# A second network for half of the rows set apart, whole VectorE operations in the last pair, and gathers that wait for the last but one

## Chip, cores and metric

One NeuronCore of one Trainium2 chip runs the whole kernel. The metric is the device time of one execution in microseconds, the median of several runs.

## What is computed

For each of 16 graphs of 1024 nodes with 64 features: normalize the rows and clip them at zero (h), drop some neighbours of nodes that have more than ten, take for every node and feature the quantiles 0.25, 0.5 and 0.75 over the neighbours that are left (itself among them), add their weighted sum to h, and put the result through two dense layers. Cut from the reference:

```
neigh = (adj_ > 0) & ~eye
rem = neigh & (sk > 1) & (rank % sk == sk - 1) & mask[:, :, None]
adj_d = jnp.where(rem | jnp.swapaxes(rem, 1, 2), 0.0, adj_)
vals = jnp.where((adj_d > 0)[..., None], x[:, None, :, :], jnp.inf)
s = jnp.sort(vals, axis=2)
for tau, w in zip((0.25, 0.5, 0.75), (0.25, 0.5, 0.25)):
    pos = tau * max(nv - 1, 0); lo, hi = floor(pos), ceil(pos)
    agg = agg + w * (v_lo + frac * (v_hi - v_lo))
y = relu((x + agg) @ W1 + b1) @ W2 + b2
```

Here x is h, nv the number of values of a node, and the layer's input is added to y at the end.

## The kernel before

**Tiling.** Nodes lie on the 128 partitions. TensorE and ScalarE turn each adjacency matrix into short lists of neighbours (`load`, `drop`, `keep`, `order`, `collect`). The nodes are put in order of their number of neighbours, so that eight tiles of 128 nodes need fewer and fewer slots (`CAPS`); `CLASSES` joins tiles with one number of lines: 13, 11, 9 and 7. Two graphs make a pair, and there are eight pairs.

**Gathers.** A slot of a tile of one graph is filled by one indirect DMA from GpSimd (POOL), L1274 in `fetch`: 128 rows of 64 floats out of a table in DRAM (`gtab`) into a tile `g`. A node without a neighbour in that slot gathers a row of the constant BIG.

**Sorting.** `sort` runs over a network written down in `PLANS`. A step is `n` pairs of lines at regular distances. With two results it is a min (L1379) and a max (L1384), each over n lines at once; with one it is L1376. An operation holds at most `PART` = 384 elements for each partition, so two lines of the 11-line class (384 elements each) go as two operations. Only those lines that can carry a quantile come out sorted (`ends`); each is multiplied by its coefficient, by VectorE at L1401 or by ScalarE at L1399 from pair `ACTP` = 3 on, and TensorE adds them up in PSUM (L1405, `acc`). From the last pair the second half is sorted for each graph by itself.

**Writes behind.** `opened` puts a write of one column (`pause`, L801) behind an operation of VectorE. A max writes over lines that its min has read; where at least one instruction stands between the two in VectorE's order, `arrange` declares that there is no dependence (`loose`), and the max need not wait.

**Rows set apart.** The 32 nodes of a graph with the most neighbours don't fit the tiles' slots. Of eight graphs, a group, they fill two rows per partition: the first (k = 0) holds nodes of up to 23 neighbours, the second (k = 1) nodes of up to `SECOND` = 14. `set_apart` copies their first slots into the tile `gg`, and `fetch_group` gathers the others (L1624). Slots that k = 1 doesn't use are filled with BIG by VectorE (L1622). `aggregate_group` sorts both rows together, 128 columns, with the 24-line network, adds the lines up in `gacc`, and goes on through the dense layers (`go`, `ot`, `gh`, `yp` at L1601, `gx`) to a scatter (L1691). There are two groups: the first is sorted in the middle of the kernel, the second ahead of the last pair. The sum of the second is also brought back into the last pair (`bring_back`, `few`).

**Order of the work.** The Python code emits the work of a pair, with the preparation of later graphs woven in (`weave`). `arrange` then takes every instruction with its dependences, gives it a cost and a lag (`Step.cost`; a write behind adds 12 ns to its operation), and plays the five queues PE, ACT, DVE, POOL and SP in time; the order found is fixed on each engine. Of several instructions that are ready the one that was emitted first goes first. `results(m)` holds the end of the work of pair m; for the last pair it starts with `aggregate_group` and the scatter, then `aggregate`. In the last pair a part of the slots (`LEAST`) is filled by TensorE (`pick`, with the one-hot tile `hot` from VectorE) and not by gathers.

Of the kernel before, what the change touches and what calls it, by code (L numbers as in the profile page):

```python
# [40 lines left out]
OP = mybir.AluOpType  # L41
# [46 lines left out]

SPREAD = 160
PART = 384  # L90


FIRST = CAPS[0] - 1
# [546 lines left out]
        return 480, 1500 + by / 300  # L640


def arrange(tc, runs, loose, tails):

    steps, found, number = [], {}, {}
    for ins in list(tc.nc.cur_bb.bb.instructions):
# [63 lines left out]
    while done < len(steps):  # L710
# [25 lines left out]
        for q in ENGINES:  # L736
            while waiting[q] and waiting[q][0][0] <= free[q]:
                heappush(able[q], heappop(waiting[q])[1])

    for steps in sequence.values():  # L740
        alike = iter(sorted((i for s in steps for i in s.tail), key=lambda i: number[i.name]))
        line = [i for s in steps for i in (s.ins, *(next(alike) for _ in s.tail))]
        at = {ins.name: k for k, ins in enumerate(line)}
        for ins in line:
            if ins.name in loose and at[loose[ins.name]] < at[ins.name] - 1:
                tc.declare_no_dep(ins, loose[ins.name], reason="read in order by one engine")
        for ins, then in zip(line, line[1:]):
            tc.add_manual_dep(
                then, ins.name, mybir.DependencyInfo(mybir.DependencyClass.NoSync, mybir.DependencyReason.DATA),
                reason="order of the engine",  # L750
            )
# [3 lines left out]
def list_layer(  # L755
# [42 lines left out]
    def opened(ins):  # L798

        at = len(tails) % 64  # L800
        tails[nc.vector.memset(pause[:, at:at + 1], 0.0).ins.name] = ins.ins.name  # L801
        return ins
# [437 lines left out]

    queue = deque()
    turn = [0]

# [17 lines left out]
    def fetch(m, classes=CLASSES, halves=(0, 1)):  # L1263

        for tiles, slots in classes:
            lo, n = tiles[0], len(tiles)
            held, order = PLANS[slots][:2]

            def begin(h, tiles=tiles, lo=lo, n=n, slots=slots, held=held):
                opening((tiles, slots), m)  # L1270
                nc.scalar.copy(gathered[m, tiles][:, slots - 1, :, h], owns[m][:, lo:lo + n, h])

            def gather(h, slot, k, at, tiles=tiles, lo=lo):
                return nc.gpsimd.indirect_dma_start(  # L1274
                    out=gathered[m, tiles][:, slot, k - lo, h], out_offset=None, in_=tables[2 * m + h][0],
                    in_offset=bass.IndirectOffsetOnAxis(ap=lists[2 * m + h][:, at:at + 1], axis=0),
                    element_offset=tables[2 * m + h][1],
                )

            for h in halves:  # L1280
                queue.append(partial(begin, h))
                for k in tiles:
                    for s, slot in enumerate(order[:FULL[k] + ((k, FULL[k]) in HOSTS)]):
                        if m < pairs - 1 or s >= LEAST[k]:
                            queue.append(partial(gather, h, slot, k, PASSED[k] + s))
# [68 lines left out]
                yield 1.0  # L1354


    def sort(lines, plan, first, coef, acc, by_act=False):

        size = prod(lines.shape[2:])

        def at(first, step, n):
            stop = first + step * (n - 1) + (1 if step >= 0 else -1)
            return lines[:, first:stop if stop >= 0 else None:step or 1]

        _, _, steps, ends, taken = plan
        most = max(1, PART // size)

        def parts(n):
            return [(k, min(most, n - k)) for k in range(0, n, most)]

        for n, a, da, b, db, f, df, back, what in steps:
            run, others = [], []
            for k, many in parts(n):
                pa, pb = at(a + k * da, da, many), at(b + k * db, db, many)
                if f < 0:
                    opened(nc.vector.tensor_tensor(pa if back else pb, pa, pb, OP.min if what == "min" else OP.max))  # L1376
                else:
                    run.append(opened(
                        nc.vector.tensor_tensor(at(f + k * df, df, many), pa, pb, OP.min if what == "<" else OP.max)  # L1379
                    ))  # L1380
            for k, many in parts(n) if f >= 0 else ():
                pa, pb = at(a + k * da, da, many), at(b + k * db, db, many)
                others.append(opened(
                    nc.vector.tensor_tensor(pa if back else pb, pa, pb, OP.max if what == "<" else OP.min)  # L1384
                ))
            loose.update((then.ins.name, ins.ins.name) for ins, then in zip(run, others))
            cost = (0.16 + n * size / 960) * (1 if f < 0 else 2)
            yield cost
        for n in taken:
            now, ends = ends[:n], ends[n:]  # L1390
            for k, many in parts(n):
                some = now[k:k + many]
                v = at(some[0], some[1] - some[0] if many > 1 else 0, many)
                v = v.rearrange("p s (k c) -> p s k c", c=C) if len(lines.shape) == 3 else v
                if by_act:
                    w = coef(first + k, many)
                    for i in range(many):
                        for j in range(v.shape[2]):
                            nc.scalar.activation(v[:, i, j], v[:, i, j], AF.Copy, scale=w[:, i, j:j + 1])  # L1399
                    continue  # L1400
                opened(nc.vector.tensor_tensor(  # L1401
                    v, v, coef(first + k, many)[:, :, :, None].to_broadcast(list(v.shape)), OP.mult
                ))
            settle([
                nc.tensor.matmul(  # L1405
                    acc, ident32, lines[:, s], start=False, stop=(s == now[-1] and not ends), skip_group_check=True
                )
                for s in now
            ])
            first += n  # L1410
            cost = 0.16 + n * size / 960
            yield cost
# [22 lines left out]
    def aggregate(m, o, between=None):  # L1435
# [4 lines left out]
        for half in (0, 1) if last else (1, 0):  # L1440
            parts = CLASSES[2 * half:2 * half + 2][::1 if last else -1]
            for sides in ((0, 1), (1, 2)) if last and half else ((0, 2),):
# [28 lines left out]
                for tiles, slots in parts:  # L1471
                    lo, n = tiles[0], len(tiles)
                    g = gathered[m, tiles]
                    plan = PLANS[slots]
                    if one is None:
                        lines, weigh = g.rearrange("p s n h c -> p s (n h c)"), partial(
                            lambda s, many, lo, n: coef[:, s:s + many, lo:lo + n].rearrange("p s n h -> p s (n h)"),
                            lo=lo, n=n,
                        )
                    else:  # L1480
                        lines, weigh = g[:, :, :, one], partial(
                            lambda s, many, lo, n, h: coef[:, s:s + many, lo:lo + n, h], lo=lo, n=n, h=one
                        )
                    yield from sort(
                        lines, plan, window(tiles, slots)[0], weigh, acc[:, lo - 4 * half:lo - 4 * half + n],
                        m >= ACTP,
                    )
                    if sides[1] == 2:
                        gathered.pop((m, tiles))
# [116 lines left out]
    def fetch_group(grp):  # L1606
# [12 lines left out]
        for k in range(n):  # L1619
            for s, slot in enumerate(s for s in PLANS[CAP][1] if s >= FIRST):  # L1620
                if k and s >= SECOND - FIRST:
                    nc.vector.memset(groups[grp][:, slot, k], BIG)  # L1622
                    continue
                nc.gpsimd.indirect_dma_start(  # L1624
                    out=groups[grp][:, slot, k], out_offset=None, in_=tab,
                    in_offset=bass.IndirectOffsetOnAxis(ap=idx[:, k, s:s + 1], axis=0),
                )
            nc.gpsimd.indirect_dma_start(
                out=xg[:, k], out_offset=None, in_=flat_x,
                in_offset=bass.IndirectOffsetOnAxis(ap=to[:, k:k + 1], axis=0),  # L1630
            )
        gathered["group", grp] = to, xg

    def aggregate_group(grp):
# [6 lines left out]
        tag, bufs = ("mx", 3) if grp == B // GROUP - 1 else ("agg", 2)  # L1641
        acc = psum.tile([P, n, C], F32, name="gacc", tag=tag, bufs=bufs)
        nc.tensor.matmul(acc, ident32, gg[:, CAP - 1], start=True, stop=False, skip_group_check=True)
        yield from sort(
            gg.rearrange("p s k c -> p s (k c)"), PLANS[CAP], window((0,), CAP)[0],
            lambda s, many: coef[:, s:s + many], acc.rearrange("p k c -> p (k c)"),
        )
        o = wk.tile([P, n * C], F32, name="go", tag="lows", bufs=1)
        nc.scalar.copy(o, acc.rearrange("p k c -> p (k c)"))
        yield 0.0  # L1650
# [144 lines left out]
                next(side)  # L1795
        weave(chain(results(m - 1) if m else (), (1.0,)), 140.0 if m else 1.0, side, 85.0 if m < pairs - 1 else 45.0)

    arrange(tc, runs, loose, tails)


def ones_col(pool, nc):
# [5 lines left out]
def window(tiles, n):  # L1807
# [56 lines left out]
        (3, 19, 2, 2, 2, 24, 1, 1, "<"), (2, 7, 3, 5, 16, 2, 4, 0, "<"), (3, 5, 10, 1, 1, 4, 3, 1, ">"),  # L1864
        (1, 20, 0, 17, 0, -1, 0, 0, "max"), (2, 0, 8, 14, -5, 2, -1, 0, ">"),
    ), (17, 9, 1, 14, 2, 15, 7, 5, 4, 24, 19, 26, 23, 25, 10, 6, 21), (3, 2, 2, 2, 2, 2, 2, 2)),
}


# [105 lines left out]
```

## Time and profile before

| | |
|---|---|
| median of 3 runs | 1521.11 us (1520.2 to 1524.35) |
| the profiled execution | 2610.97 us, span 2609.2 us |
| mean granted TensorE clock in it | 0.709 |
| PE, PEld busy | 1220.6, 756.3 us |
| DVE (VectorE) busy | 1224.7 us |
| ACT (ScalarE) busy | 1111.4 us |
| POOL (GpSimd) busy | 966.4 us, 952 + 26 + 4 gathers and 4 scatters among it |
| writes behind (L801) | 2237, 59 ns each as recorded |

The span is the time from the first to the last instruction of one profiled execution; 1.8 us lie around it. That execution took 1.72 times the median of the runs without a profile, so its durations of single instructions can be used, and its idle times only with care. [...]the distance from start to start says what an operation costs in a row of them.

### The profile page before, as it was taken

To read this page: it belongs to the slowest core of one execution; us is meant where nothing else is said; L and a number is where in the kernel's file an instruction comes from. 1 tells how busy PE (TensorE), PEld (TensorE's weight loads), DVE (VectorE), ACT (ScalarE), POOL (GpSimd) and SP (SyncE) were. 2 spreads that over 40 slices of the span, in tenths; PEclk is the share of its full clock that TensorE was granted. 3 is DMA by queue.
4 is the path that set the end of the run, shared out by engine and by line. 5 is a ranking of instruction groups with operands and counts; after the bars stand their busy time and mean duration, and the time that the engine had idled before them with its cause. 6 is when DMAs were issued, how large, how long until landed. Compare 5 with 4: busy or idle time off the path is not lost.

```text
span 2609.2 us, 29583 instructions
## 1 busy us (share of the span) xinstructions
PE 1220.6 (47%) x8971; PEld 756.3 (29%) x8971; DVE 1224.7 (47%) x5963; ACT 1111.4 (43%) x3089; POOL 966.4 (37%) x995
## 2 busy tenths in 40 slices
PE   6144246154807192253816427145392254655536
PEld 4133134032404151142413214033251122353223
DVE  5123168043508371383507704088374171449496
ACT  6244146143606271343606626055482254315355
POOL 1724431653272527324370154702507434420400
PEclk9567578576958595585957758577596566876668
DMA  5222122121213121221212112121212010100100
GB/s 171 62 77 68 39 56 73 33 58 45 56 34 86 28 70 32 62 52 50 59 26 80 42 19 59 26 65 33 51 54 50 16 21 16 32 13 3 22 9 11
DMA packets 128826, 121.62 MB, mean 47 GB/s; under 512 B 95730, under 2 KB 96274, under 8 KB 128658
## 3 DMA queue, kind: packets, MB, share of 16 engines
q1 hardware_dynamic: 97106, 87.29, 11.3%
q0 software_dynamic: 31552, 32.36, 6.4%
q8 instruction: 72, 1.18, 0.2%
q14 instruction: 96, 0.79, 0.1%
HBM read 108.79 MB, written 9.05 MB: 45 GB/s over the span
## 4 chain that ended last, share of the span: by engine, by line
another core or an unknown queue 27%; PE 17%; ACT 17%; issue 16%; DVE 6%; DMA 0%; DVEq 0%; ACTq 0%
PE codeP L1090 3%; PE acc L1405 3%; ACT dist L993 2%; ACT g L1399 2%; ACT kept L1016 2%; ACT sg L906 2%; DVE g L1384 1%; ACT ne L926 1%; PE tp L913 1%; DVE g L1379 1%; PE rk L988 1%; PE rk L983 1%; PE got L1341 1%; ACT waste L1188 1%
## 5 line engine op out<-in xcount | busy, mean ns | idle before, releaser
L1274 POOL DMA_INDIRECT g<-gtab,idx x952 | 921.0, 967 | 1373.9 <-issue 307.7
L1384 DVE TENSOR_TENSOR g<-g 128x256 f32<-128x256 f32 (+1 forms) x675 | 312.0, 484 | 39.0 <-remote 26.6
L1379 DVE TENSOR_TENSOR g<-g 128x256 f32<-128x256 f32 (+1 forms) x675 | 312.8, 486 | 28.8 <-remote 18.9
L993 ACT ACTIVATE dist<-rk,bias 128x512 f16<-128x512 f32 x256 | 170.2, 696 | 314.4 <-remote 215.0
L983 PE MATMUL rk<-kb,cnt 128*128 128x512 bf16 x256 | 121.4, 474 | 349.0 <-ACT dist L993 166.9
L926 ACT ACTIVATE ne<-tp 128x512 fp8e4<-128x512 f32 x248 | 141.0, 605 | 280.3 <-remote 226.3
L994 DVE TENSOR_SCALAR rem<-dist,half 128x1024 bf16<-128x1024 f16 x128 | 63.0, 493 | 402.6 <-ACT dist L993 351.7
L913 PE MATMUL tp<-kb,sg 128*128 128x128 bf16 x1024 | 118.4, 258 | 285.2 <-ACT sg L906 114.7
L988 PEld LDWEIGHTS <-ne 128*128 128x128 fp8e4 x1024 | 97.7, 117 | 414.4 <-issue 396.9
L1090 PE MATMUL codeP<-pack,perm 128*128 128x332 bf16 x1024 | 195.1, 333 | 11.2 <-DVE perm L1065 8.7
L913 PEld LDWEIGHTS <-sg 128*128 128x128 bf16 x1024 | 89.5, 118 | 309.0 <-issue 172.1
L1016 ACT ACTIVATE kept<-kp 128x512 fp8e4<-128x512 f32 x224 | 134.2, 615 | 91.8 <-remote 54.1
L1405 PE MATMUL acc<-g,kf 128*128 128x128 f32 (+2 forms) x472 | 141.2, 432 | 64.5 <-ACT g L1399 45.3
L1399 ACT ACTIVATE g<-g,coef 128x64 f32<-128x64 f32 x560 | 147.5, 350 | 52.2 <-DVE g L1379 21.0
L801 DVE MEMSET pause<- 128x1 bf16 x2237 | 132.0, 59 | 7.0 <-issue 7.0
L988 PE MATMUL rk<-kw,ne 128*128 128x128 fp8e5 x1024 | 128.7, 258 | 0.0
L906 ACT ACTIVATE sg<-at 128x1024 bf16<-128x1024 f32 x121 | 126.5, 1070 | 3.4 <-DMA at<-in_adj_dram 3.4
L1105 DVE MAX8 keys<-codeP 128x8 f32<-128x128 f32 x128 | 38.0, 297 | 186.7 <-ACT own L1100 145.1
L1090 PEld LDWEIGHTS <-perm 128*128 128x128 bf16 x1024 | 97.2, 105 | 89.3 <-DVE perm L1065 25.1
L1511 DVE TENSOR_SCALAR at_p<-iota,node 128x512 bf16<-128x512 f16 x208 | 66.8, 357 | 100.0 <-remote 57.4
L1019 PE MATMUL code<-kw,kept 128*128 128x17 fp8e5 x1024 | 65.5, 173 | 98.9 <-issue 56.6
L1405 PEld LDWEIGHTS acc<-g,kf 128*128 128x128 f32 x472 | 83.4, 218 | 90.0 <-ACT g L1399 57.1
(205 smaller groups left out, 2533.5 us busy)
## 6 DMA issues: line engine op xcount, KB each, us to landing
at<-in_adj_dram SPq DMA_DIRECT2D x122, 512.0 KB
g<-gtab,idx POOLq DMA_INDIRECT x952
xt<-in_x_dram SPq DMA_DIRECT2D x16, 256.0 KB
y<-in_x_dram SPq DMA_DIRECT2D x16, 256.0 KB
gtab<-xt SPq DMA_DIRECT2D x16, 256.0 KB
out_dram<-y SPq DMA_DIRECT2D x14, 256.0 KB
spare<-in_adj_dram SPq DMA_DIRECT2D x6, 512.0 KB
gg<-g SPq DMA_DIRECT2D x32, 48.0 KB
```

The costliest lines, as they stand in the source:

```text
L906: nc.scalar.activation(sg, at, AF.Sign)
L913: run.append(nc.tensor.matmul(tp[:, s], sg[:, m * P:(m + 1) * P], ident16, start=(s == 0), stop=(s == 3 and t // 4 != n), skip_group_check ...
L926: nc.scalar.activation(to, tp, AF.Relu, saturate=False)
L988: run.append(nc.tensor.matmul(rk[:, s * P:(s + 1) * P], ne[:, 4 * n + s, ts], upper, start=False, stop=(s == 3), skip_group_check=True,))
L993: nc.scalar.activation(dist[:, n * HALF:(n + 1) * HALF], rk, AF.Abs, bias=bias[:, t:t + 1])
L1016: nc.scalar.activation(kept[:, 4 * n:4 * n + 4], kp, AF.Relu, saturate=False)
L1090: run.append(nc.tensor.matmul(flat, perm[:, t, k * P:(k + 1) * P], pack[:, t], start=False, stop=(t == NT - 1), skip_group_check=True,))
L1274: return nc.gpsimd.indirect_dma_start(out=gathered[m, tiles][:, slot, k - lo, h], out_offset=None, in_=tables[2 * m + h][0], in_offset=bas ...
L1379: nc.vector.tensor_tensor(at(f + k * df, df, many), pa, pb, OP.min if what == "<" else OP.max)
L1384: nc.vector.tensor_tensor(pa if back else pb, pa, pb, OP.max if what == "<" else OP.min)
L1399: nc.scalar.activation(v[:, i, j], v[:, i, j], AF.Copy, scale=w[:, i, j:j + 1])
L1405: nc.tensor.matmul(acc, ident32, lines[:, s], start=False, stop=(s == now[-1] and not ends), skip_group_check=True)
```

## The change

Four things are done.

- The two rows set apart are sorted one after the other in the code, k = 1 first, each over its own 64 columns: k = 1 with a network of 15 lines that uses the slots of the 24-line plan, k = 0 with the 24-line one. The slots that k = 1 doesn't use are no longer filled with BIG.
- In the sorts of the last pair and of the second group an operation may hold `WHOLE` = 1024 elements, and no write stands behind it.
- Each gather of `fetch` adds one to a semaphore when GpSimd has finished it[...]. In the order that `arrange` found, gather k waits until k - 1 of them have done so, that is, until gather k - 2 is through. Gathers of a group and scatters neither wait nor count.
- The sums of the two rows go to their halves of `gacc` separately.

The new network: 26 steps, of two results 1 x 6 pairs, 1 x 4, 3 x 3, 16 x 2, and 5 steps of one result; 10 lines come out, two at a time.

```diff
 PART = 384
+WHOLE = 1024
...
-def arrange(tc, runs, loose, tails):
+def arrange(tc, runs, loose, tails, paced):
...
+    for k, s in enumerate(s for s in sequence["POOL"] if s.ins.name in paced[1]):
+        if k > 1:
+            paced[1][s.ins.name].wait_op(paced[0], k - 1, "sem-ge")
...
+    paced = nc.alloc_semaphore("issued"), {}
...
             def gather(h, slot, k, at, tiles=tiles, lo=lo):
-                return nc.gpsimd.indirect_dma_start(
+                ins = nc.gpsimd.indirect_dma_start(
...
-                    element_offset=tables[2 * m + h][1],
+                    element_offset=tables[2 * m + h][1], engine_sem=issued,
                 )
+                given_out[ins.ins.name] = ins
+                return ins
...
-    def sort(lines, plan, first, coef, acc, by_act=False):
+    def sort(lines, plan, first, coef, acc, by_act=False, whole=False):
...
-        most = max(1, PART // size)
+        most = max(1, (WHOLE if whole else PART) // size)
+        gap = (lambda ins: ins) if whole else opened
...
-                    opened(nc.vector.tensor_tensor(pa if back else pb, pa, pb, OP.min if what == "min" else OP.max))
+                    gap(nc.vector.tensor_tensor(pa if back else pb, pa, pb, OP.min if what == "min" else OP.max))
...
                     yield from sort(
                         lines, plan, window(tiles, slots)[0], weigh, acc[:, lo - 4 * half:lo - 4 * half + n],
-                        m >= ACTP,
+                        m >= ACTP, last,
                     )
...
                 if k and s >= SECOND - FIRST:
-                    nc.vector.memset(groups[grp][:, slot, k], BIG)
                     continue
...
-        yield from sort(
-            gg.rearrange("p s k c -> p s (k c)"), PLANS[CAP], window((0,), CAP)[0],
-            lambda s, many: coef[:, s:s + many], acc.rearrange("p k c -> p (k c)"),
-        )
+        for k in range(n)[::-1]:
+            yield from sort(
+                gg[:, :, k], PLANS[(CAP, SECOND + 1)[k]], window((0,), CAP)[0],
+                lambda s, many: coef[:, s:s + many, k:k + 1], acc[:, k], whole=grp == B // GROUP - 1,
+            )
...
-    arrange(tc, runs, loose, tails)
+    arrange(tc, runs, loose, tails, paced)
...
+    15: (27, (), (
+        (6, 1, 2, 0, 2, 14, 1, 1, "<"), (4, 15, 2, 14, 2, 2, 2, 1, ">"), (3, 11, 6, 9, 6, 22, -4, 1, "<"),
...
+    ), (12, 15, 13, 21, 11, 26, 22, 20, 5, 18), (2, 2, 2, 2, 2)),
```

The min, the max and the multiplication of `sort` all go through `gap` in place of `opened`; the lines left out do that.

## The prediction

> **What bounds the kernel now.** I read the totals first, then the costliest groups, then stretches of the span, then the chain that ended last. The totals show no engine that is full:
>
> ```profile
> PE 1220.6 (47%) x8971; PEld 756.3 (29%) x8971; DVE 1224.7 (47%) x5963; ACT 1111.4 (43%) x3089; POOL 966.4 (37%) x995
> L1274 POOL DMA_INDIRECT g<-gtab,idx x952 | 921.0, 967 | 1373.9 <-issue 307.7
> L801 DVE MEMSET pause<- 128x1 bf16 x2237 | 132.0, 59 | 7.0 <-issue 7.0
> ```
>
> The profiled execution took 2610.97 us for a span of 2609.2, 1.72 times the median of 1521.11. So shares of its span can't be read as shares of a normal run. Stretches show why (columns: stretch, its length, busy PE, PEld, DVE, ACT, POOL, granted clock, DMA share, GB/s):
>
> ```profile
> 1520.00:1540.00 20.00, 1.57 (x10) 0.71 (x10) 0.00 (x0) 1.07 (x3) 15.12 (x17) 0.50 0.15 27
> 1740.00:1760.00 20.00, 0.00 (x0) 0.00 (x0) 19.64 (x99) 0.00 (x0) 0.00 (x0) 0.50 0.00 0
> 2500.00:2520.00 20.00, 0.00 (x0) 0.00 (x0) 20.00 (x93) 15.85 (x27) 0.00 (x0) 0.50 0.00 1
> 2520.00:2540.00 20.00, 4.04 (x19) 4.05 (x20) 20.00 (x97) 0.00 (x0) 0.00 (x0) 0.50 0.00 0
> 2540.00:2560.00 20.00, 13.98 (x52) 8.93 (x52) 16.26 (x78) 13.33 (x54) 1.94 (x2) 0.78 0.01 4
> ```
>
> While POOL issues gathers in a row (first line), the others nearly stop; when it rests they fill up. A normal run can't be like that: gathers, and the others' work after them, would not fit into 1521 us. There the two must overlap. What each costs is still readable. Gathers are paced by start to start:
>
> ```profile
> 2442.98 0.95 POOL L1274 DMA_INDIRECT g<-gtab,idx  x1 [0.30 <-issue]
> 2444.24 0.94 POOL L1274 DMA_INDIRECT g<-gtab,idx  x1 [0.30 <-issue]
> 2445.48 0.95 POOL L1274 DMA_INDIRECT g<-gtab,idx  x1 [0.30 <-issue]
> ```
>
> 1.25 us each. The 952 gathers with the 26 + 4 of the groups make 982 x 1.25 = 1228 us. The first starts at 69.7 us and some 125 to 160 us of work follow the last (161 here, of which up to 35 are the stop beside the last gathers). 70 + 1228 + 125 to 160 = 1423 to 1458 of the 1521: **in the middle POOL is over nine tenths full, and the end is DVE's.** From 2320 to 2588 DVE is the full engine except beside the last 32 gathers; from 2460 to 2544 it is busy 77.7 of 84 us, with no gather left. The chain that ended last goes through DVE's sorting to 2535.9, then:
>
> ```profile
> 2535.96 6.98 PE gacc L1405 x34
> 2546.65 0.76 PE yp L1597 x4
> 2547.50 0.31 DVE yp L1601
> ```
>
> So DVE work taken out of the last 150 us is worth nearly its own length; after DVE's last sort operation (2588.4) a fixed 20.8 us follow.
>
> [...]operations start 0.212, 0.345 and 0.479 us apart at 128, 256 and 384 elements, that is elements/0.96 + 78 ns, the small write behind included; 256-element ones without it start 0.33 apart (L1602 to the next). The write behind costs about 13 ns, not the 59 of its row. [...]in the first group's sort, alone on DVE, the max starts 0.48 after the min, but the next min, which needs that max, starts 0.59 after it:
>
> ```profile
> 1742.75 0.56 DVE L1379 TENSOR_TENSOR gg<-gg 128x384 f32<-128x384 f32 x1
> 1743.23 0.55 DVE L1384 TENSOR_TENSOR gg<-gg 128x384 f32<-128x384 f32 x1
> 1743.82 0.56 DVE L1379 TENSOR_TENSOR gg<-gg 128x384 f32<-128x384 f32 x1
> ```
>
> I take 0.11 us for a dependence that nothing fills.[...]
>
> **The change, part by part.**
>
> *Group sort.* Before, the 24-line network works on both set-apart rows, 128 columns. From the rows of gg (halved, there are two groups): 64 operations of 384, 28 of 256, 3 of 128, and 1 + 7 multiplications: 65 x 0.479 + 35 x 0.345 + 3 x 0.212 = 43.8 us. After, the same 103 operations have 64 columns, and the 15-line network adds 47 operations and 5 multiplications. In the last group without writes behind (elements/0.96 + 65 ns): 24 lines: 65 x 0.265 + 35 x 0.198 + 3 x 0.132 = 24.6; 15 lines: 2 x 0.465 + 2 x 0.332 + 6 x 0.265 + 37 x 0.198 + 5 x 0.132 = 11.2. Sum 35.8: **8.0 us less**. The two networks touch different columns, so each fills the other's handovers. The nine BIG memsets per group go: 9 x 0.112 = 1.0 us less. Sums on PE: 27 lines of 64 columns for 17 of 128, 54 records for 34; at 0.12 to 0.24 us (the 128x64 records of L1597) 6.5 to 13 us against 7.0, but 20 of them belong to the short network and can run while the long one sorts. Behind it 34 stay: nothing.
>
> *First group.* With writes behind it saves about 43.8 - 37.8 + 1.0 = 7 us of DVE. It lies in the stretch where POOL's gathers set the pace; I take 0, with 0 to 7 for the range.
>
> *Whole operations in the last pair.* Only the 11-line class is cut at PART: 64 operations of 384 and 3 more before, 32 of 768 (0.865 each) and 3 after: 32.1 to 29.1, 3.0 less. The 13-line class loses 34 writes, the two sides of the 9- and 7-line classes 88: 122 x 0.013 = 1.6 less. Multiplications there are ACT's and stay.
>
> *What it gives back.* Without the write, a min and its max stand next to each other whenever nothing else is ready, and then the max waits for the min, 0.11 us, where before no wait was declared. Beside another sort it costs nothing. Alone are the last six steps of the 9-line network (15 steps against 9) on each side: 12 x 0.11 = 1.3 us. The 11-line class alone would lose what merging gave: four 0.479 operations or two of 0.865 + 0.11, 1.92 or 1.95 a step; half of it has the group beside it and the rest can have the next side's networks.
>
> *Pacing.* [...]Behind a waiting gather stand the later gathers, group gathers and scatters in POOL's queue; the sorts wait for them. While k waits, k-1 still has about 1.25 us to run, and a semaphore is seen here within 0.02 to 0.12 us ("issue" pieces of the chain), so the wait should end in time. Nor does the distance of gathers hang on how many are queued: at 69.7 us, after 47 idle us, it is 1.48, 1.26, 1.25, the same as 100 gathers later. Bounds: 0 if hidden; if an increment comes into the distance, 0.04 us x 952 = 38 us; below nothing if it is the run ahead that stops the other engines. I take 0. SP's transfers and their order are not touched.
>
> *Sum.* 8.0 + 1.0 + 3.0 + 1.6 - 1.3 = 12.3 us off DVE's last stretch. Against the profiled 2610.97 that is 2598.7; its excess lies beside gathers, so I subtract the same from the median: 1521.1 - 12.3 = **1508.8, say 1509 us**. The written-out order is planned anew with these costs, which I give 6 us either way. DVE's idle 3.5 us ahead of yp (L1601) probably stays: that result is late next, and PE's 7 us behind the group were planned shorter.
>
> **Rivals.**
> - *The gain doesn't arrive.* DVE falls idle where it now works: on yp, on ACT's coefficients (36 in 8.7 us from 2550.5), and on min to max. For it: ACT and PE carry half of the chain after 2536. Against: ACT idles 26.7 us before go. About 1519.
> - *Pacing slows POOL.* In the middle POOL is nearly full, so every ns on a gather is 0.95 us of the kernel; from 13 ns on it eats the gain of the end. At 0.04 us: 1509 + 36 = 1545. Against: the wait can be hidden, as above.
> - *Pacing frees the others.* If the stops beside gather bursts exist, smaller, in normal runs, and come from queued gathers, POOL's 63 to 98 idle us (1521 less 1423 to 1458) shrink by half: about 1470. Against: pairs already overlap.
> - That the change doesn't do what it says can't be for the networks, whose operations are counted in the plans; for the pacing it can: if POOL never holds more than two gathers, the wait changes nothing.
>
> **How the numbers follow.** Forecast 0.62 (1503 to 1515), no gain 0.15, slower POOL 0.13, freed engines 0.10. A measurement here can tell about 0.3%, 4.6 us. Faster by more: 0.62 and the 0.10, less and plus small edges, 0.73; within: 0.13; slower: 0.14. The range 1482 to 1530 leaves out most of freed engines and the upper part of slower POOL, under 2 in 10.
>
> **What would show it.** Right: gg operations of 192, 128 and 64 columns and a group sort near 36 us of DVE; 32 g operations of 768; about 240 fewer writes behind (103 + 189 go, 52 come with the first group); gathers still 1.25 apart; the span after the last gather shorter by some 12 us. Wrong: gathers 1.27 or more apart, min to max 0.11 longer through most of the last pair, or longer idle ahead of L1601.

## Result and profile after

The changed kernel takes 1514.23 us (median of 17 runs, 1510.99 to 1518.03), the kernel before beside it 1518.84 us (17 runs): a ratio of 0.9971, interval 0.9959 to 0.9983. That is 4.6 us gained where 12.3 were forecast. The profiled execution of after has a span of 1511.7 us at a granted clock of 0.864. The 2610.97 us of the execution that the prediction read are like what one chip gave in every run: the kernel before took 2645.2 us (median of 62 runs) on the chip that ran h1 to h4 below, and 1517.6 to 1519.2 us on the four others.

Totals and costliest group from the page of after (busy us, share of the span, instructions; then busy us, mean ns, idle time before and what ended it):

```profile
PE 1147.9 (76%) x9011; PEld 724.0 (48%) x9011; DVE 1213.6 (80%) x5777; ACT 1099.5 (73%) x3089; POOL 1044.7 (69%) x995
L1281 POOL DMA_INDIRECT g<-gtab,idx x952 | 995.4, 1046 | 351.8 <-DMA g<-gtab,idx 284.5
```

Groups of after, shapes kept apart:

```profile
L805 DVE MEMSET pause<- 128x1 bf16 x1997 | 117.8, 59 | 0.0
L1394 DVE TENSOR_TENSOR gg<-gg 128x192 f32<-128x192 f32 x70 | 24.4, 350 | 0.2
L1389 DVE TENSOR_TENSOR gg<-gg 128x192 f32<-128x192 f32 x70 | 24.3, 351 | 0.3
...
L1394 DVE TENSOR_TENSOR g<-g 128x768 f32<-128x768 f32 x16 | 15.2, 949 | 0.0
L1389 DVE TENSOR_TENSOR g<-g 128x768 f32<-128x768 f32 x16 | 15.2, 949 | 0.0
```

So the change did what it says: operations of gg with 192 columns instead of 384, 32 of g with 768, and 240 fewer writes behind (2237 to 1997). The distance from one gather to the next has the forecast 1.25 us as its median, but many distances are longer, as the first two here:

```profile
1326.10 1.08 POOL L1281 DMA_INDIRECT g<-gtab,idx  x1 [0.30 <-DMA g<-gtab,idx]
1327.49 1.07 POOL L1281 DMA_INDIRECT g<-gtab,idx  x1 [0.30 <-DMA g<-gtab,idx]
1328.86 0.94 POOL L1281 DMA_INDIRECT g<-gtab,idx  x1 [0.30 <-DMA g<-gtab,idx]
```

They are 1.37 to 1.39 apart here and 1.35 on average (1046 ns and 0.30), so POOL issues almost without a pause from 70 us to its last list gather (a gather of `fetch`) at 1412.6. The chain that ended last, behind the second group:

```profile
1441.18 0.36 DVE gg L1411
1441.58 7.53 PE gacc L1415 x34
...
1453.57 0.76 PE yp L1607 x4
1454.42 0.30 DVE yp L1611
```

From the multiplication at its head to yp this chain takes 13.2 us, PE's sum of 34 records being 7.5 of it, and DVE stands idle for the last 5.2 us of that.

### The profile page after: what moved, and what is told of

Its sections match the earlier page's. It is cut to its first block, busy times and chain, and to the rows that moved or that the text cites. A ratio compares the mean times of both kernels' runs of the same rounds, so it can differ in the third digit from the quotient of the medians.

```text
span 1511.7 us, 30392 instructions
## 1 busy us (share of the span) xinstructions
PE 1147.9 (76%) x9011; PEld 724.0 (48%) x9011; DVE 1213.6 (80%) x5777; ACT 1099.5 (73%) x3089; POOL 1044.7 (69%) x995
## 5 line engine op out<-in xcount | busy, mean ns | idle before, releaser
L1281 POOL DMA_INDIRECT g<-gtab,idx x952 | 995.4, 1046 | 351.8 <-DMA g<-gtab,idx 284.5
L1389 DVE TENSOR_TENSOR g<-g 128x256 f32<-128x256 f32 (+3 forms) x659 | 310.2, 492 | 13.5 <-PE acc L1460 8.5
L1394 DVE TENSOR_TENSOR g<-g 128x256 f32<-128x256 f32 (+3 forms) x659 | 308.4, 490 | 3.6 <-PE acc L1460 1.9
L1094 PE MATMUL codeP<-pack,perm 128*128 128x332 bf16 x1024 | 187.7, 325 | 12.1 <-DVE perm L1069 11.5
L987 PE MATMUL rk<-kb,cnt 128*128 128x512 bf16 x256 | 114.0, 445 | 69.4 <-ACT dist L997 65.1
L917 PE MATMUL tp<-kb,sg 128*128 128x128 bf16 x1024 | 109.8, 246 | 70.5 <-ACT sg L910 55.3
L992 PE MATMUL rk<-kw,ne 128*128 128x128 fp8e5 x1024 | 119.7, 245 | 0.0
L805 DVE MEMSET pause<- 128x1 bf16 x1997 | 117.8, 59 | 0.0
L1099 ACT CAST st<-codeP 128x4 bf16<-128x4 f32 x128 | 21.5, 168 | 124.0 <-PE codeP L1094 123.8
L1015 PE MATMUL kp<-kw,rem 128*128 128x128 fp8e5 x1024 | 100.1, 219 | 0.0
L1010 PE MATMUL kp<-ne,kw 128*128 128x512 fp8e4 x256 | 98.9, 387 | 0.5 <-ACT kept L1020 0.4
```

What stands on the lines that cost most here:

```text
L917: run.append(nc.tensor.matmul(tp[:, s], sg[:, m * P:(m + 1) * P], ident16, start=(s == 0), stop=(s == 3 and t // 4 != n), skip_group_check ...
L992: run.append(nc.tensor.matmul(rk[:, s * P:(s + 1) * P], ne[:, 4 * n + s, ts], upper, start=False, stop=(s == 3), skip_group_check=True,))
L1094: run.append(nc.tensor.matmul(flat, perm[:, t, k * P:(k + 1) * P], pack[:, t], start=False, stop=(t == NT - 1), skip_group_check=True,))
L1281: ins = nc.gpsimd.indirect_dma_start(out=gathered[m, tiles][:, slot, k - lo, h], out_offset=None, in_=tables[2 * m + h][0], in_offset=bass ...
```

## Experiments

All ratios are to the kernel before on the same chip. Except for h1 to h4, 1 us is 0.00066. Line numbers are those of each run's own kernel; they are those of after, or up to 8 more behind an edit. The two networks always come without the BIG fills of the group concerned.

**The parts alone: e1 to e4.** e1 is before with the pacing only, e2 after without it:

```diff
-                    element_offset=tables[2 * m + h][1],
+                    element_offset=tables[2 * m + h][1], engine_sem=issued,
...
+        if k > 1:
+            paced[1][s.ins.name].wait_op(paced[0], k - 1, "sem-ge")
```

> The kernel before with the pacing alone. Theory A (pacing is free in a normal run, the end gave only part of its gain): within 2 us of the kernel before, about 1519, and its profiled execution takes about 1517 us and not 2611, because queued gathers only disturb an execution with a profile. Theory B (pacing costs POOL 8 us, which hides a gain of 12 at the end): about 1527, gathers further apart than 1.35 us. The profile of this kernel is also the first undisturbed one of the work before: theory A expects the sort of the second group to end about 73 us ahead of the end, as in the disturbed profile.

> The changed kernel without the pacing (no wait, no increment). Theory A: about 1514, as with it, and a profiled execution near 2600 us. Theory B: about 1507. A theory C, that pacing helps a normal run: 1519 or more.

Measured: e1 0.9991 (0.9975 to 1.0007); e2 1514.32 us, 0.9968 (0.9957 to 0.998), where after has 1514.23. Pacing is worth nothing that shows, either way. Nor do the profiles show a price for POOL. A gather takes 1046 ns on average in after and 1038 in e1, but the kernels without pacing on these chips lie between 1026 (i2) and 1069 (f1), and the median gather takes 0.95 us with pacing and without (after, e2). The averages differ by a few long gathers; more on them below. In e1 the last operation of the second group's sort starts 72.8 us ahead of the end, near the 73 of theory A. The other half of the expectation of e2 missed: its profiled execution took 1510.79 us, no 2600.

e3 is before with the two networks only, e4 before with the whole operations and without the writes behind only:

```diff
+        for k in range(n)[::-1]:                                    # e3
+            yield from sort(gg[:, :, k], PLANS[(CAP, SECOND + 1)[k]], ...)
...
-        most = max(1, PART // size)                                 # e4
+        most = max(1, (WHOLE if whole else PART) // size)
+        gap = (lambda ins: ins) if whole else opened
```

> The kernel before with the 15-line network for the second rows alone (both groups; writes behind and PART kept, no pacing). 7 us less DVE work at the last group, 7 at the first. Theory A: 2 to 4 us faster than before, since DVE then waits longer for yp behind the group; full arrival would be 8 us faster.

> The kernel before with whole operations and no writes behind in the last pair and the last group alone (no network, no pacing). 4.6 us less DVE in the last pair and 1.3 in the group, less up to 3 us for min to max waits. Theory A: 0 to 2 us faster; full arrival 5 us faster; if the waits between min and max rule, 1 to 3 us slower.

Measured: e3 1520.98 us, 1.0016 (1.0007 to 1.0026), slower by 2.5 us; e4 1511.29 us, 0.9954 (0.9941 to 0.9967), faster by 7.0. Both expectations missed, in opposite directions. The part that was to bring most costs time, and the small part alone ends up 3.0 us below e2 beside it (2.1 by the ratios): it is the version to take. DVE's busy time did fall as planned: 1232.9 us in e1, 1219.7 in e3, 13.2 less.

**Which of e4's edits: f5, f6.** f5 leaves out the merging, f6 keeps the writes behind:

```diff
-        most = max(1, (WHOLE if whole else PART) // size)           # f5
+        most = max(1, PART // size)
...
-        gap = (lambda ins: ins) if whole else opened                # f6
+        gap = opened
```

> e4 without its merging: in the last pair and the last group no write behind an operation, but operations still cut at 384 columns. Splits e4's 7.0 us. By the prediction's prices: 295 writes fewer at 13 ns is 3.8 us, less up to 1.3 us of waits of max for min: 2.5 to 3.8 us below the kernel before (1514.5 to 1516). If a write behind costs nothing on the path (a rival), 0 to 1 us.

> e4 with its writes behind kept: only the 11-line class of the last pair is done in operations of 768 columns instead of two of 384. By the prediction's prices 3.0 us of DVE less, up to 1 us given back where min and max stand next to each other: 2 to 3 us below the kernel before (1515.3 to 1516.3). If its place is hidden beside the group's sort (a rival): 0 to 1 us.

Measured: f5 0.9972 (0.996 to 0.9984), 4.3 us; f6 0.9964 (0.9946 to 0.9983), 5.5 us. Both halves count. Each brings more than was expected of it, though the intervals (about 2 to 6, and 3 to 8 us) reach into what was expected. Their sum is above e4's 7.0, but the intervals allow that they add up.

**Which group's network: f1, f2.** Both are e4 with the network in one group:

```diff
+        if grp == B // GROUP - 1:      # f1; f2: grp < B // GROUP - 1
+            for k in range(n)[::-1]:
+                yield from sort(gg[:, :, k], PLANS[(CAP, SECOND + 1)[k]], ...)
+        else:
+            yield from sort(gg.rearrange("p s k c -> p s (k c)"), PLANS[CAP], ...)
```

> Whole operations in the last pair as in e4, and the 15-line network in the last group only; the first group is sorted as before, so the order of all work up to 1340 us stays that of e4. Theory D (the order): the network's 8 us were lost twice, the larger part at 1340 to 1360 us, where the last pair's first gathers wait for the pair before to be sorted, which the first group's new order set back by 9 us; without that the last group's 8 us arrive but for 2 to 3 us of longer idle ahead of yp. Then 1505 to 1508, 3 to 6 us below e4's 1511.3. Theory E (the chain behind the group, on PE and ACT, sets the end whatever the group's sort takes): no faster than e4, 1510 to 1515.

> As e4, with the 15-line network in the first group only. Theory D: the first group's sort takes 7 us less DVE time and yet the kernel is 3 to 5 us slower than e4, 1514 to 1516, with DVE's sort of the second last pair ending 6 to 9 us later (ACT's run of 24 coefficients near 1330 instead of 1325 us) and POOL waiting 4 to 16 us for it near 1350. Theory E: no effect, 1510 to 1513.

Measured (us, and the ratio to the kernel before beside it; first group across, last group down; no pacing, whole operations throughout; e4 and e2 ran on one chip, f1 and f2 on another):

| | first group: one network | first group: two networks |
|---|---|---|
| last group: one network | e4 1511.29, 0.9954 | f2 1525.85, 1.0032 |
| last group: two networks | f1 1511.35, 0.9953 | e2 1514.32, 0.9968 |

The parts don't add up: the last group's network is worth 0 beside an old first group and 10 to 11.5 us beside a new one (by ratios, by medians); the first group's costs 2 to 3 us, which the intervals don't tell from nothing, or 12 to 14.6. The recorded ratio of f2 (1.0016 to 1.0048) is lower than that of its medians, 1.0047, hence the ranges. Theory E is right for f1, theory D for f2 in direction only, the loss being at least twice what it gave.

*Where f1 loses its gain.* The group's last multiplication starts at 1453.2 us in e4 and at 1430.7 in f1, 22.5 earlier. DVE's last sort operation ends at 1489.7 and 1485.0, only 4.7 earlier, and the span is 1509.6 and 1507.8, 1.8 shorter. Between these two points of the group and the last sort operation DVE stands idle for 5.3 us in e4 and 12.3 in f1; behind the last sort operation follow 19.9 us in e4 and 22.9 in f1. The timelines of f1, DVE first, then PE:

```profile
1436.96 1.29 DVE L1389 TENSOR_TENSOR g<-g 128x256 f32<-128x256 f32 x2
1443.50 0.30 DVE L1611 TENSOR_TENSOR yp<-yp,gapart 128x128 f32<-128x128 f32 x1 [5.26 <-PE yp L1607]
1443.71 0.95 DVE L1394 TENSOR_TENSOR g<-g 128x768 f32<-128x768 f32 x1
...
1460.61 0.28 DVE L1704 TENSOR_TENSOR few<-few,o 32x128 f32<-32x128 f32 x1 [4.09 <-ACT o L1702]
...
1486.31 5.43 PE L1415 MATMUL acc<-g,kf 128*128 128x128 f32 x24 [4.55 <-ACT g L1409]
```

and of e4:

```profile
1464.49 0.30 DVE L1611 TENSOR_TENSOR yp<-yp,gapart 128x128 f32<-128x128 f32 x1 [2.44 <-ACT g L1409]
...
1490.35 3.10 PE L1415 MATMUL acc<-g,kf 128*128 128x128 f32 x24 [0.92 <-ACT g L1409]
```

In f1 yp stands in DVE's fixed order ahead of the last two operations of the 11-line class, which need nothing from it. DVE waits 5.26 us, and ACT's multiplications, PE's sums and the last pair's first output stand behind those two. It waits another 4.09 us for `few`, the group's sum on its way back into the last pair. Later the last 24 sums take 5.43 us instead of 3.10. The stretches show why (last column but two: granted clock). f1:

```profile
1485.00:1490.00 5.00, 3.69 (x17) 3.69 (x18) 0.00 (x0) 2.93 (x13) 0.00 (x0) 0.50 0.00 0
```

e4:

```profile
1485.00:1490.00 5.00, 4.42 (x24) 1.96 (x22) 4.08 (x13) 2.42 (x11) 0.00 (x0) 1.00 0.21 52
```

PE had waited 4.55 us in f1 and runs at half clock; in e4 other matmuls ran until 0.92 us before, and the clock is full. The mean clock of f1 is 0.97 from 1480 to 1485 us, so by an estimate from this and the 0.50 behind it the clock halved about 3 us into the gap, which begins at 1481.76. The length of a gap alone doesn't tell, though: in e4 the 24 sums from 1472.74 us took 4.62 us behind a wait of only 1.8, at a mean clock of 0.82 from 1470 to 1480 us (worked out from 0.91 over 1470 to 1490 and 1.00 from 1480). So the earlier end of the group's sort opened gaps, and the last sums, behind the one of 4.55 us and at a clock of 0.50, took 2.3 us longer. The seen parts add up: of 4.7 us at the last sort operation 4.0 are left at the start of these sums, 1.7 at their end and 1.8 in the span. That the sums would be faster without the gap was not tried by itself.

*Where f2 loses.* Up to 1260 us DVE has begun nearly as many operations on g in f2 as in f1 (1219 and 1223). At 1320 it is 27 behind (1310 and 1337). Its waits from 1252 to 1322, and POOL's from 1340 to 1380:

```profile
DVE hot L1341 <- ACT rows L1337: 5.2, 1, 5.2
DVE g L1389 <- ACT g L1362: 4.3, 1, 4.3
DVE g L1480 <- ACT g L1477: 2.5, 1, 2.5
...
POOL g L1281 <- ACT g L1409: 6.6, 1, 6.6
```

f1 has only the first of these waits of DVE there, 4.5 us, with another of 0.5. In f1 operations of sorting stand ready in the order between two runs of `hot`; in f2 they stand behind a picked line (L1362) that isn't there yet. This is the setback that the expectations speak of. POOL's last gathers then wait for the pair before to be sorted (up to 15.8 us in e2), and the group's last multiplication starts at 1460.8 instead of e4's 1453.2, 7.6 later. DVE's last sort operation then ends 11.2 us later than in e4, and the span is 14.5 longer; what adds the rest was not followed up.

*Is it POOL?* In f1 the gathers beside the group's sort become long, which no expectation had:

```profile
1378.11 5.94 POOL L1281 DMA_INDIRECT g<-gtab,idx  x1 [0.30 <-issue]
...
1388.21 9.02 POOL L1281 DMA_INDIRECT g<-gtab,idx  x1 [0.30 <-issue]
...
1423.81 1.03 POOL L1281 DMA_INDIRECT g<-gtab,idx  x1 [0.30 <-issue]
```

The last one starts 31 us later than in e4 (1392.7). All six kernels that sort the last group with two networks and no writes behind (after, e2, f1, and f4, i1, p2 below) have three to ten gathers of over 1.5 us among their last 60; of the nine others on these chips only f3 has one. Neither part alone does it: e3 keeps the writes behind, e4 the one network, and both have none. Why this is so was not tested. It isn't what holds the end up: from 1360 us on DVE waits for no gather in f1, and in f4, whose last gather starts 21.7 us earlier than f1's, the time is no shorter.

**Is it the order? f3, f4, p1, p2.** f3 is e4, f4 is f1, with a longer cost for the group's sum in the planner; p1 is e4, p2 is e2, with every DVE operation 2 ns longer in it. No instruction changes:

```diff
                 busy = 60 + n if n < 512 else 850                   # f3, f4
+                if self.writes[0].tile.name.startswith("gacc") and self.writes[0].tile.tag == "mx":
+                    busy = 360
...
-            return (most + 66) / 0.96 + (60 if psum else 0), 80     # p1, p2
+            return (most + 68) / 0.96 + (60 if psum else 0), 80
```

> As e4, but the planner takes 0.41 us for each fp32 matmul of the last group's sum (as measured: 34 records in 7.0 us for 17), where it took 0.22; so yp and what follows the group are planned 3 us later. The computation is the same. Theory D: idle ahead of yp falls from 2.4 us to under 1 and the time falls by 0 to 2 us (1509 to 1511). Theory E: no effect of over 1 us either way.

> f1 and f3 together. Theory D: what f1 loses to idle ahead of yp comes back: 2 to 3 us below f1, 1503 to 1506. Theory E: as f1, within 1 us.

> e4 with the same instructions in another order: the planner takes each DVE operation to be 2 ns longer, which moves nothing but ties and near ties. Theory D, in its strong form (which order comes out is worth several us, whatever the change): 2 us or more from e4's 1511.3, either way. Rival (the order is robust; the loss at 1340 us belongs to the network): within 1.5 us of e4.

> The changed kernel without pacing (e2, 1514.3) with the same instructions in another order, by the same 2 ns in the planner. Theory D, strong form: 2 us or more from e2, either way, most likely faster, since the setback at 1340 us is bad luck of one order. Rival: within 1.5 us of e2, with POOL's wait near 1350 us still there.

Measured: f3 0.9954 (0.9934 to 0.9973), f4 0.9963 (0.9945 to 0.9981), p1 0.9942 (0.9922 to 0.9961), p2 0.9952 (0.9936 to 0.9968). None can be told from the kernel that it was made from (e4 0.9954, f1 0.9953, e2 0.9968). In f3 DVE's idle time ahead of yp stays at 2.5 us, where under 1 was expected. In f4 the wait ahead of yp is still 5.3 us: the longer cost didn't move yp behind the two operations, so f4 doesn't tell what that wait is worth. In p2 the setback is still there: POOL is busy 4.2 of the 20 us from 1340 to 1360, as in e2 (3.6). These small shifts of the order are worth nothing that shows, and the one in p2 doesn't remove the setback. A thoroughly different order was not tried.

**Is it ACT? h1 to h3, i1, i2.** h1, h2 and i1 are f1, h3 and i2 are e4, with the multiplications of the last pair moved from ACT to DVE, in h1 all, in the others those of the last two classes; h4 is e2 with the next graphs' preparation woven in faster:

```diff
-                        m >= ACTP, last,
+                        m >= ACTP and not (last and half), last,    # h1: and not last
...
-        weave(..., side, 85.0 if m < pairs - 1 else 45.0)           # h4
+        weave(..., side, 80.0 if m < pairs - 1 else 45.0)
```

> f1 with all multiplications of the last pair done by DVE in whole operations instead of by ACT row by row (0.24 us for 64 columns of one row there). Theory F (after the group, the last pair's chain through ACT's multiplications and PE's sums sets the end): DVE has 22 us idle from 1440 to 1500 in f1, so it takes this work into its gaps and the chain shortens: 3 to 8 us below f1's 1511.35. Rival G (DVE's sorting of the last pair sets the end even so): slower than f1 by the added DVE work, 5 to 10 us.

> As h1, but DVE multiplies only in the last two classes (9 and 7 lines, each side by itself); the 13- and 11-line classes stay with ACT. Theory F: 3 to 6 us below f1. Rival G: 2 to 5 us slower than f1.

> h2's edit on e4, where the last group is sorted by one network as before and ends 21 us later. Theory F: DVE is the full engine there until 1460 us, so the same edit brings less than on f1: within 2 us of e4's 1511.3. If it brings as much as on f1, the group's end has no part in it.

> The changed kernel without pacing (e2) with the same instructions; the next images' preparation is woven in faster (its full length counted as 80 instead of 85), which moves work of the first 1350 us about. Theory D (the setback at 1260 to 1340 us is a matter of the written order): the waits there change and the time moves by 4 us or more from e2's 1514.3, either way. Rival (it belongs to the network): within 2 us of e2, POOL's wait of 12 to 16 us near 1350 still there.

> The same kernel as h2: f1 with the last two classes of the last pair multiplied by DVE in whole operations instead of by ACT row by row. Theory F (ACT's multiplications and PE's sums of the last pair set the end): 3 to 6 us below f1, ratio to the kernel before 0.991 to 0.9935 where f1 had 0.9953. Rival G (DVE's sorting sets it even so): slower than f1 by 2 to 5 us, 0.997 or more.

> The same kernel as h3: i1's edit on e4, without the 15-line network. Theory F: DVE is full there until 1460 us, so little comes of it: 0.994 to 0.9965 where e4 had 0.9954; i1 is then 3 us or more faster than i2, which is what the network's 8 us in the last group are worth once the chain behind it is shorter. Rival: i1 and i2 within 1.5 us.

h1 to h4 ran on the chip on which the kernel before takes 2645.2 us: h1 0.9975 (0.9965 to 0.9985), h2 0.9954 (0.9935 to 0.9973), h3 0.9977 (0.9962 to 0.9991), h4 0.9988 (0.9976 to 0.9999). Without their bases beside them they don't decide what they were made for; h4 settles nothing. i1 and i2 ran on a chip like the first ones: i1 0.9959 (0.9944 to 0.9974), i2 0.9964 (0.9951 to 0.9977). Theory F expected 0.991 to 0.9935 for i1 and falls: without ACT's share the end stays where it was. Rival G expected 0.997 or more, which i1's ratio doesn't bear out either, though its interval just reaches there. i1 and i2 lie 1.2 us apart, as the rival of i2 expected, not 3. The chain of i1:

```profile
1485.58 0.95 DVE g L1411 x2
1486.57 5.46 PE acc L1415 x24
```

DVE's multiplications end at 1486.5; in f1 ACT's ended at 1487.9, and in f1 the sums followed them line by line from 1486.3. PE's 24 sums at half clock begin at the same time in both. The wait ahead of yp is 5.3 us again, and the last pair's first half reaches its output at 1459.1 (1458.8 in f1).

**What stays open.** e4, f1, f3, p1 and i1 all lie between 1510.9 and 1511.7 us. That the length of DVE's work there sets this end, or ACT's multiplications alone, is not borne out: taking away the one (f1) or moving the other (i1) left it in place. The waits ahead of yp and `few` and PE's half clock are seen in the traces, but they were not taken away, so that they hold the end up is argued. Where the first group's network loses was located, at 1260 us; why it leads to the worse order there was not explained.

## Why the prediction was right or wrong

**Direction and range** held: faster, and 1514.2 lies within 1482 to 1530. The size was 2.7 times too large, and the gain has another source than the forecast. Of its 12.3 us, 4.6 were for whole operations and 7.7 for the networks. Measured are 7.0 for the whole operations (e4), and a loss of 2 to 3 us for both networks together (e4 to e2, or e3 alone). That the sum came out on the right side owes something to luck.

**Step that failed: "DVE work taken out of the last 150 us is worth nearly its own length".** The group sort of both groups lost 13.2 us of DVE's busy time in e3, which keeps the writes behind; the prediction's 43.8 - 37.8 + 1.0 = 7 for such a group makes 14 for two, so the sizing was fair. Its value was not: f1 against e4 brings nothing in the last group, where 7.7 us were expected. In the profile DVE looked full in front of the group's end; behind it the last pair needs ACT, PE and DVE in turn, and with less of the group's sort left to lay between, DVE's idle time there grew from 5.3 to 12.3 us. The 20.8 us behind the last sort operation weren't fixed either: 19.9 in e4, 22.9 in f1 with PE at half clock. Beside the first group's new network the same step brings 10 to 11.5 us (f2 to e2), so its worth hangs on the order around it, not on its length.

**"Idle 3.5 us ahead of yp probably stays"** failed too: 3.4 us in e1, 6.2 in e3, 5.2 in after, 5.3 in f1. With less of the group's work left there was less to lay between, while PE's 34 records ahead of yp still took 7.5 us (7.0 before). The rival "the gain doesn't arrive" named this wait; its size, about 1519, is near that of the networks alone (e3, 1521), though not of the change.

**First group: "I take 0, with 0 to 7 for the range".** It costs 2 to 3 us beside the last group's new network (f1 to e2; not clear of noise) and about 12 or more without it (e4 to f2), through the setback above. The range excluded a loss, with the reason that the stretch is POOL's; but the order is fixed for all engines at once, and a shorter step early moves what stands behind it.

**Whole operations: 3.0 + 1.6, 1.3 given back, and 103 x 0.013 = 1.3 of writes behind in the group, thus 4.6.** Measured 7.0 (5.0 to 9.0): the mechanism is right and the term was somewhat small. The price of missing writes is there. The timeline of after, where the group sorts alone, shows min and max 0.39 us apart at 192 columns, 0.12 above the 0.265 of the prediction:

```profile
1411.91 0.36 DVE L1389 TENSOR_TENSOR gg<-gg 128x192 f32<-128x192 f32 x1
1412.30 0.36 DVE L1394 TENSOR_TENSOR gg<-gg 128x192 f32<-128x192 f32 x1
1412.69 0.36 DVE L1389 TENSOR_TENSOR gg<-gg 128x192 f32<-128x192 f32 x1
```

From 1411.5 to 1417.2 us nothing stands between the two. Later, with an operation of 768 columns of g between two of gg, the next operation starts 0.27 us behind one of 192 columns (whose own record is 0.35 us long), so there the two sorts fill each other's waits, as expected.

**Pacing: 0** was right (e1, and after against e2). That the median gather takes 0.95 us with it and without fits the wait being hidden. The rival's sentence "every ns on a gather is 0.95 us of the kernel" is wrong here: in f1 a gather takes 40 ns more on average than in e4 and the last one starts 31 us later, and the end did not move. (Its 0.04 us a gather was the author's assumption, shown by no trace; times 952 it makes 38 us, as in the bounds, not 36.) 1.25 us from gather to gather is right as a median, but the mean is 1.33 to 1.37 in e1 to e4, f1 and after. So the sign "1.27 or more apart" can't tell what pacing does: e2, without it, has 1.34.

## What to carry over

Time that a step saves on the busiest engine counts only as far as the work behind it can start earlier (in f1 22.5 us at the group's end left 1.8 of the span): look for what stands behind it in each engine's fixed order (here yp ahead of two ready operations) and for the clock that PE has behind a gap (0.50 behind 4.55 us in f1), and test the step alone before pricing it. In a schedule that is fixed for all engines, a saving early in the kernel has no safe sign (f2 came out 14.6 us above e4); the range needs a loss as well. When a profiled execution is far from the median of the runs, take from it the counts and the order, and keep durations and overlaps in doubt.

## What was not expected of the hardware

- The same program took 1518 us on four chips and 2645 us on a fifth. There gathers were shorter (963 ns in h4, 1046 in after), but POOL and the other engines took turns: h2 shows POOL waiting 113 us for PE between two gathers, and from 2460 to 2480 us POOL busy for 15.1 of 20 us where PE is for 4.6 and DVE for 2.4.
- 24 fp32 sums took 3.10 us in e4 at a granted clock of 1.00, and 5.43 us in f1, where it was 0.50 behind 4.55 us without work.
- Beside a sort of 64-column rows without writes behind, single gathers took up to 9.0 us on POOL in f1 (9.4 in p2) instead of 0.95; with the writes (e3), or with 128 columns (e4), none did.
